# A four-layer graph network on one core: layer 1's ends cut finer, layer 2's first block as a dense sum

## The chip, the cores and the metric

One core of a Trainium2 chip runs the whole program. The metric is the device time of one execution in microseconds; of several runs the median is given. The profile shows one execution, taken by the hardware profiler, and its time differs from the median of the runs.

## The reference

2708 nodes with 512 features each, and one sparse matrix `adj` of 2708 x 2708 (a diagonal, and some four neighbours in a row). Four layers follow each other, each a residual and a layer norm. What matters here are layers 1 and 2:

```python
def layer1(x, adj):                       # attention over neighbours, and a plain sum
    t  = adj @ x
    ga = sigmoid([t, x] @ Wa.T + ba);  gb = sigmoid([t, x] @ Wb.T + bb)
    h  = x @ W_sa
    e  = where(adj != 0, exp(-leaky_relu(s_left(h)[:, None] + s_right(h)[None, :], 0.01)), 0)
    return sigmoid(ga * ((e / (e.sum(1) + 1e-5)) @ h) + gb * (adj @ (x @ W_gcnb) + b_gcnb))

def layer2(x, adj):                       # weighted incidence
    head = (adj > 0) / max(sqrt((adj > 0).sum(1)), 1e-12)
    inc  = adj + head
    return (inc @ x) / inc.sum(1)

x = layernorm(x + layer0(x, adj))         # residual sum with a dense projection
x = layernorm(x + layer1(x, adj))
x = layernorm(x + layer2(x, adj))
x = layernorm(x + layer3(x, adj))         # degree-normed sum, projection, tanh
```

## The kernel before

Rows of the result are worked off in NB = 24 blocks of R = 113 rows (the last has 109). Layer 0 reads the whole of `adj`, block by block, and writes a list of the non-zero entries: for each block up to EC x 128 = 512 edges in four **chunks** of 128 edges, with the source node (`source`), row and value of each. From then on a sum over neighbours is done in two steps. `gather` (L602) issues four indirect DMAs on POOL for a block, one for each chunk, which fetch the rows of the source nodes from a table in device memory into one of three buffers `gath` (block i uses buffer i % 3). Then TensorE multiplies: a chunk's edge values, spread to a 128 x 113 matrix, against the chunk's fetched rows, summed over the four chunks in PSUM (`aggregate`, L614). The diagonal is kept apart and added from the block's own rows.

Each layer's result is written to a table (`table[1]` after layer 1) by DMAs from the SP queue, and the next layer's gathers wait until the table is complete, since a source may be any node.

The order of instructions on each engine is written out by hand: every engine takes its instructions strictly in the order of the program text, and waits by semaphores where an operand is late. So a call's place in the text is its place in the queues of all the engines that it uses. A buffer ring (`bufs=`) makes a write wait for the readers of the tile that had the place before.

The parts of layer 1 for block i, with their engines:

- `gather1(i)`: four gathers of 1029 columns on POOL from `table[0]`. `load_own1(i)` (L648) loads the block's own rows by SP for the first nine blocks, `gather_own1(i)` (L1394) by one indirect DMA on POOL for those after.
- `values1(i, chunks)`: ScalarE spreads the edge values (`edge_s`).
- `scores1(i)` (L1421): two VectorE steps and an exp on ScalarE on a [128, 4, 113] tile. They need all four chunks. `mask1(i)` (L1432) zeroes what is no edge. `s_left` (L1377, L1383) holds the left scores of all blocks, spread over the partitions by transposes on TensorE and a VectorE copy for four blocks at once; all six are made before the loop.
- `sums1(i)` (L1436) and `scored_sums1(i)` (L1446): 8 matmuls each, two column halves of four chunks, half after half; `l1s` and `l1e` in the profile.
- `gates1`, `gated1`, `both1` (L1482), `stats1` (L1504), `scale1`, `norm1`: VectorE and ScalarE, with a small power on POOL (L1523); `norm1` stores the block to `table[1]`.
- `source_sum(i)` (L1349): one VectorE step for the degrees that layer 3 needs; it uses `in_block` and `block_of`. `row_norms` (L1592) makes the norm of the rows for layer 2: three VectorE steps and a power on POOL.

The loop interleaves blocks: in turn i it gathers block i + 2, sums block i, finishes block i - 1 and scores block i + 1.

Between the layers: `turn_norm` and `copy_norm` spread a row norm over the partitions (TensorE, ScalarE), `values` (L1304) and `incidence` (L1622) make the edge weights of layer 2 on VectorE for blocks 0 and 1, `keep_warm` (L1579) issues matmuls whose result is not read, and a chain of small VectorE steps (L1697 to L1730) makes the row sums and degrees. Then layer 2 gathers blocks 0 and 1 (L1714), and its loop runs over the 24 blocks: gather of block i + 2, `aggregate` of block i (`l2a`), `stats2` and `norm2` of block i - 1, `values` and `incidence` of block i + 2. `own2(i)` makes the block's own part, which has the diagonal and the residual.

Of the kernel before, what the change touches and what calls it, by code (L numbers as in the profile page):

```python
# [12 lines left out]
P = 128  # L13
# [6 lines left out]
EC = 4  # L20
# [427 lines left out]
def sparse_stack(  # L448
# [213 lines left out]
    with ExitStack() as phase:  # L662
# [635 lines left out]
        for i in range(7, NO):  # L1298
            load_own1(i)
# [29 lines left out]
    for k, t in enumerate((ba_bc, bb_bc)):  # L1329
# [7 lines left out]
    in_block = gpool.tile([P, NB, NS], I32, name="in_block")  # L1337
    nc.vector.tensor_scalar(
        in_block, where_all, 1.0 / R, 0.5 / R - 0.5, op0=ALU.mult, op1=ALU.add
    )  # L1340
    block_of = gpool.tile([P, NB, NS], FP, name="block_of")
    for g, (c0, _) in enumerate(SEGS):
        at = slice(8 * g, 8 * g + 8)
        nc.vector.tensor_scalar(
            block_of[:, :, at], in_block[:, :, at], float(c0), None, op0=ALU.add
        )
# [74 lines left out]
    def scores1(i):  # L1421

        e = spool.tile([P, EC, R], FP, tag="e", name=f"e{i}")
        nc.vector.tensor_tensor(
            e, gath[i % NGB][:, :, SR : SR + 1].to_broadcast([P, EC, R]),
            over_chunks(s_left[:, i, :]), ALU.add,
        )
        nc.vector.scalar_tensor_tensor(e, e, 0.01, e, op0=ALU.mult, op1=ALU.max)
        nc.scalar.activation(e, e, AF.Exp, scale=-1.0)
        edge_e[i] = e  # L1430

    def mask1(i):  # L1432
        e = edge_e[i]
        nc.vector.scalar_tensor_tensor(e, edge_s[i], 0.0, e, op0=ALU.is_gt, op1=ALU.mult)

    def sums1(i):  # L1436
        g, s, r = gath[i % NGB], edge_s.pop(i), rows(i)
        sum_s[i] = ps_1s.tile([P, 2, D], FP, tag="s1", name=f"l1s{i}")
        for k, at in enumerate(s_at):
            for c in range(EC):  # L1440
                nc.tensor.matmul(  # L1441
                    sum_s[i][:r, k, : at.stop - at.start], lhsT=s[:, c, :r], rhs=g[:, c, at],
                    start=(c == 0), stop=(c == EC - 1),
                )

    def scored_sums1(i):  # L1446
        g, e, r = gath[i % NGB], edge_e.pop(i), rows(i)
        sum_e[i] = ps_1e.tile([P, 2, D], FP, tag="e1", name=f"l1e{i}")
        for k, at in enumerate(e_at):
            for c in range(EC):  # L1450
                nc.tensor.matmul(  # L1451
                    sum_e[i][:r, k, k : k + at.stop - at.start], lhsT=e[:, c, :r],
                    rhs=g[:, c, at], start=(c == 0), stop=(c == EC - 1),
                )
# [27 lines left out]
    def both1(i):  # L1482
# [9 lines left out]
        nc.vector.scalar_tensor_tensor(  # L1492
            halves(va, r), halves(own1.pop(i)[:, 1 : D + 1], r), ediag[:r, i : i + 1],
            agg[:r, :, 1 : H + 1], op0=ALU.mult, op1=ALU.add,
        )
        v = work.tile([P, D], FP, tag="v", name=f"l1v{i}")
        nc.vector.scalar_tensor_tensor(
            v[:r, :], va[:r, :], rec[:r, :], vb1.pop(i)[:r, :], op0=ALU.mult, op1=ALU.add
        )

        nc.scalar.activation(v[:r, :], v[:r, :], AF.Tanh, scale=0.5)
        v1[i] = v

    def stats1(i):  # L1504
        r, v = rows(i), v1[i]
        nc.vector.scalar_tensor_tensor(
            v[:r, :], v[:r, :], 0.5, xr[:r, i, :], op0=ALU.mult, op1=ALU.add
        )
        stats = small.tile([P, 6], FP, tag="stats", name=f"st_l1_{i}")
        nc.vector.bn_stats(stats[:r, :], v[:r, :])  # L1510
# [4 lines left out]
        nc.vector.bn_aggr(mv[:r, k, 0:2], stats[:r, :])  # L1515
# [74 lines left out]
    nc.vector.tensor_scalar(plus, adiag, 0.0, None, op0=ALU.is_gt)  # L1590
# [17 lines left out]
    row_in, inc2 = {}, {}  # L1608
# [21 lines left out]

    b3_bc = gpool.tile([P, D], FP, name="b3_bc")
# [4 lines left out]
    gather1(1)  # L1636
    values1(1, range(EC))
    for i in range(0, NB, 4):
        spread_left(i)
    spread_bias(bg_bc)  # L1640
    scores1(0)
    mask1(0)
    for i in range(NB):
        if i + 2 < NB:
            gather1(i + 2)
        sums1(i)
# [4 lines left out]
        scored_sums1(i)  # L1651
        if i + 1 == NB:
            turn_norm(0)
            turn_norm(1)
        if i + 1 < NB:
            scores1(i + 1)
# [17 lines left out]
        if i + 1 == NB:  # L1674
            nc.sync.dma_start(out=b3_bc[0:1, :], in_=b3[None, :])
            nc.sync.dma_start(out=w3_sb, in_=w3T.rearrange("(b p) o -> p b o", p=P))
        if i < KB:
            source_sum(i)
        if i == KB:
            source_sums_out()  # L1680
            row_norms(slice(0, KB))
    copy_norm(0)
    copy_norm(1)
    keep_warm(ps_sp, "sp", [P, 4, P], 8)
    both1(NB - 1)
    spread_row(b3_bc, "b3")
    stats1(NB - 1)
    scale1()
    norm1(NB - 1)
    deg_ps = source_sums_in()  # L1690
    inc_s = [values(0)]
    incidence(0, inc_s[0])
    inc_s.append(values(1))
    incidence(1, inc_s[1])
# [11 lines left out]
    phase.close()  # L1706
    ps_agg = ctx.enter_context(tc.tile_pool(name="ps_agg2", bufs=2, space=bass.MemoryType.PSUM))
    ps_tr = ctx.enter_context(tc.tile_pool(name="ps_tr2", bufs=1, space=bass.MemoryType.PSUM))
    ps_o = ctx.enter_context(tc.tile_pool(name="ps_o2", bufs=2, space=bass.MemoryType.PSUM))
    ps_sp = ctx.enter_context(tc.tile_pool(name="ps_sp2", bufs=2, space=bass.MemoryType.PSUM))  # L1710
    ps_u = ctx.enter_context(tc.tile_pool(name="ps_u", bufs=1, space=bass.MemoryType.PSUM))


    for i in range(2):  # L1714
# [210 lines left out]
```

## Time and profile before

| | |
|---|---|
| median of 3 runs | 973.66 us (972.88 to 977.18) |
| the profiled execution's own time | 958.69 us |
| its span | 956.9 us |
| busy: TensorE, VectorE, ScalarE, POOL | 884.8, 685.3, 526.3, 465.5 us |
| layer 0 | to about 410 us |
| layer 1 | first gather 414.26, last norm ends 615.2 |
| layer 2 | first gather 618.51, last matmul ends 753.9 |
| layer 3 | first gather 760.79, to the end |

Times in the traces are microseconds from the start of the span. A row of a timeline has the start, the duration (us), the engine (PE is TensorE, DVE VectorE, ACT ScalarE, POOL GpSimd), the line of the kernel, the operation, the output and inputs by name, the count of instructions merged in the row, and in brackets the idle time before with what ended it. A 32-bit matmul is recorded as two passes, so x8 are four matmuls. A row of DMA_INDIRECT is the issuing of a gather on POOL, not its transfer; that ends some microseconds later ("to landing").

### The profile page before, as it was taken

The numbers are of one execution on the slowest core, as the hardware profiler recorded it, in microseconds if no ns is written. First come the engines' busy times: TensorE is split into PE (matmuls) and PEld (weight loads), VectorE is DVE, ScalarE is ACT, GpSimd is POOL, SyncE is SP. The second block draws the span as 40 slices with busy tenths as digits, with TensorE's granted clock in tenths as the row PEclk, the third lists the DMA queues.
The fourth block names the chain that finished last, engine by engine and source line by source line (L and its number), as shares of the span: only waits on it lengthen the run. The fifth ranks groups of instructions, "written<-read, shape, count | busy, mean of one in ns | idle before, by whom it ended". The sixth has DMA issues, their size and how long they took to land.

```text
span 956.9 us, 11163 instructions
## 1 busy us (share of the span) xinstructions
PE 884.8 (92%) x2957; PEld 489.4 (51%) x2957; DVE 685.3 (72%) x1811; ACT 526.3 (55%) x1221; POOL 465.5 (49%) x518
## 2 busy tenths in 40 slices
PE   6889999999999999989999999798888899999993
PEld 2446565556565565557777777433233334444441
DVE  7788798888888853148999999777777436565553
ACT  5776676867677672347777777344544312222221
POOL 3323131432323230057777753377777477766630
PEclk7879999999999999989999999989999999999997
DMA  9986887988878454388999976367777466555531
GB/s 245 323 208 184 216 229 207 272 223 220 227 206 238 152 166 126 115 286 292 349 330 342 341 276 236 95 188 213 212 218 217 131 170 189 163 174 162 151 107 32
DMA packets 133717, 201.73 MB, mean 211 GB/s; under 512 B 82658, under 2 KB 82704, under 8 KB 133647
## 3 DMA queue, kind: packets, MB, share of 16 engines
q0 software_dynamic: 39024, 118.69, 40.2%
q1 hardware_dynamic: 94623, 82.25, 30.2%
q8 instruction: 26, 0.43, 0.2%
q14 instruction: 44, 0.36, 0.1%
HBM read 182.81 MB, written 27.80 MB: 220 GB/s over the span
## 4 chain that ended last, share of the span: by engine, by line
PE 58%; DMA 14%; DVE 14%; issue 5%; ACT 4%; SPq 3%; POOL 2%; POOLq 0%; DVEq 0%; ACTq 0%
PE o_l L588 15%; DMA gath<-table,source 11%; PE l3a L617 8%; PE hb L588 7%; PE h L588 7%; PE l0a L617 6%; PE l2a L617 2%; PE fetched L929 2%; POOL gath L604 2%; PE unread L1585 2%; DVE l1b L1471 1%; SPq L691 1%; DMA gath<-in_x_dram 1%; DVE l1b L1475 1%; DVE l1a L1492 1%
## 5 line engine op out<-in xcount | busy, mean ns | idle before, releaser
L604 POOL DMA_INDIRECT gath<-table,source x288 | 305.0, 1059 | 102.7 <-issue 49.0
L604 POOL DMA_INDIRECT gath<-in_x_dram,source x96 | 97.4, 1015 | 224.9 <-issue 190.7
L617 PE MATMUL l2a<-gath,s_left 128*113 128x512 f32 (+1 forms) x192 | 97.2, 624 | 17.6 <-DMA gath<-table,source 17.4
L1451 PE MATMUL l1e<-gath,e 128*113 128x257 f32 (+3 forms) x384 | 88.4, 383 | 10.4 <-DVE l1a L1492 10.4
L617 PE MATMUL l3a<-gath,s 128*113 128x512 f32 (+1 forms) x192 | 88.3, 603 | 2.7 <-DMA gath<-table,source 2.7
L1441 PE MATMUL l1s<-gath,s 128*113 128x256 f32 (+3 forms) x384 | 89.8, 387 | 0.0
L617 PE MATMUL l0a<-gath,s 128*113 128x512 f32 (+1 forms) x192 | 87.5, 596 | 0.1
L588 PE MATMUL o_l<-shared,xi_own 128*113 128x512 f32 (+1 forms) x192 | 86.5, 593 | 0.8 <-ACT xi_own L581 0.7
L588 PE MATMUL hb<-w_gc_sb,xi_own 128*128 128x512 f32 (+1 forms) x176 | 83.3, 601 | 0.0
L1451 PEld LDWEIGHTS l1e<-gath,e 128*113 128x113 f32 (+1 forms) x384 | 66.2, 177 | 32.7 <-PE l1s L1441 19.4
L588 PE MATMUL o_l<-w_sb,uw_own 128*128 128x512 f32 (+1 forms) x176 | 82.7, 614 | 0.2
L588 PE MATMUL h<-w_sa_sb,xi_own 128*128 128x259 f32 (+1 forms) x352 | 80.8, 382 | 0.0
L1441 PEld LDWEIGHTS l1s<-gath,s 128*113 128x113 f32 (+1 forms) x384 | 69.2, 181 | 17.8 <-ACT s L1416 1.5
L588 PEld LDWEIGHTS h<-w_sa_sb,xi_own 128*128 128x128 f32 (+1 forms) x352 | 64.8, 185 | 19.8 <-issue 6.1
L617 PEld LDWEIGHTS l2a<-gath,s_left 128*113 128x113 f32 (+1 forms) x192 | 30.4, 181 | 73.9 <-DMA gath<-table,source 53.9
L1844 ACT ACTIVATE y<-l3v,mv_l 113x512 f32<-113x512 f32 (+1 forms) x24 | 19.5, 813 | 86.2 <-DVE mv_l L1840 79.2
L588 PEld LDWEIGHTS o_l<-shared,xi_own 128*113 128x113 f32 (+1 forms) x192 | 33.9, 177 | 49.2 <-issue 47.1
L617 PEld LDWEIGHTS l0a<-gath,s 128*113 128x113 f32 (+1 forms) x192 | 33.5, 179 | 40.7 <-issue 35.5
L617 PEld LDWEIGHTS l3a<-gath,s 128*113 128x113 f32 (+1 forms) x192 | 32.5, 180 | 41.2 <-issue 37.9
L1818 DVE SCALAR_TENSOR_TENSOR l3v<-o_l,d_inv,b_bc 113x512 f32<-113x512 f32 (+1 forms) x25 | 18.1, 728 | 48.1 <-PE o_l L588 48.1
L1308 DVE TENSOR_SCALAR s<-niota_r,nrow,edges 128x113 f32<-128x113 f32 x192 | 51.5, 344 | 0.0
L876 DVE FIND_INDEX8 where_all<-rec_all,shared 128x8 uint32<-128x678 f32 (+1 forms) x64 | 51.2, 800 | 0.0
(256 smaller groups left out, 1580.6 us busy)
## 6 DMA issues: line engine op xcount, KB each, us to landing
shared<-in_adj_dram SPq DMA_DIRECT2D x14, 1186.5 KB
table<-st SPq DMA_DIRECT2D x21, 514.5 KB
gath<-in_adj_dram SPq DMA_DIRECT2D x7, 1186.5 KB
gath<-in_x_dram SPq DMA_DIRECT2D x21, 256.0 KB
xi_own<-in_x_dram SPq DMA_DIRECT2D x23, 224.0 KB
table<-xr SPq DMA_DIRECT2D x23, 224.0 KB
table<-y SPq DMA_DIRECT2D x23, 224.0 KB
out_dram<-y SPq DMA_DIRECT2D x23, 224.0 KB
```

The lines of the kernel that those rows point to most:

```text
L588: nc.tensor.matmul(o, lhsT=uT[:, f, :r], rhs=w[:, f, :], start=(f == 0), stop=(f == DB - 1))
L604: nc.gpsimd.indirect_dma_start(out=g[:, c, :n], out_offset=None, in_=src[:, :], in_offset=bass.IndirectOffsetOnAxis(ap=source[:, i, c : c ...
L617: nc.tensor.matmul(agg[:r, :], lhsT=s[:, c, :r], rhs=g[:, c, off : off + D], start=(c == 0), stop=(c == EC - 1),)
L691: nc.sync.dma_start(out=a[:TAIL, NF, :r], in_=adjT[NF * P :, at])
L876: nc.vector.max_index(out=where_all[:, i, g * 8 : (g + 1) * 8], in_max=top, in_values=seg)
L929: nc.tensor.matmul(t["fetched"][:, c, : 3 * NS], lhsT=t["q"][:, c * P : (c + 1) * P], rhs=rec_all[:, i].rearrange("p k s -> p (k s)"), sta ...
L1308: nc.vector.tensor_scalar(s[:, c, :], niota_r, nrow[:, i, c : c + 1], edges[:, i, c, 1:2], op0=ALU.is_equal, op1=ALU.mult,)
L1441: nc.tensor.matmul(sum_s[i][:r, k, : at.stop - at.start], lhsT=s[:, c, :r], rhs=g[:, c, at], start=(c == 0), stop=(c == EC - 1),)
L1451: nc.tensor.matmul(sum_e[i][:r, k, k : k + at.stop - at.start], lhsT=e[:, c, :r], rhs=g[:, c, at], start=(c == 0), stop=(c == EC - 1),)
L1585: nc.tensor.matmul(o[:, :cols], lhsT=ident, rhs=bg_bc[:, :cols], start=True, stop=True)
L1818: nc.vector.scalar_tensor_tensor(v[:r, at], o[:r, at], d_inv[:r, i : i + 1], b3_bc[:r, at], op0=ALU.mult, op1=ALU.add,)
L1844: nc.scalar.activation(y[:r, :], v[:r, :], AF.Identity, bias=mv[:r, 3:4], scale=mv[:r, 2:3])
```

## The change

It has five parts.

1. **Start of layer 1.** The own rows of blocks 7 and 8 are no longer loaded by SP at the end of layer 0, but by `gather_own1` on POOL after the gathers of block 1. For block 0 `scores1` and `mask1` are called twice, for two chunks each, and the matmuls of `sums1` and `scored_sums1` go chunk by chunk, both halves of a chunk after each other. `in_block`, `block_of` and `plus` are made later, and two matmuls that nobody reads are added.
2. **`spread_left` late.** Only the first two of six calls stay ahead of the loop; the others are made in turns 1 to 4 of the loop.
3. **End of layer 1.** In turn 22 `load_all` loads the first 113 columns of the transposed `adj` (what block 0 needs, from all 2708 sources) by six SP DMAs into `xi_own` and `uw_own`, whose own rows are done with. Row norm of block 0: `row_norms(slice(0, 1))` at the end of turn 20, `turn_norm(0)` and `copy_norm(0)` in turn 21.
4. **Last block of layer 1 by halves:** `both1` and `stats1` work on two column halves of 256.
5. **Layer 2's first block.** `incidence_all` turns the loaded columns into weights on VectorE, four nodes' blocks at a time, and `sums_all` multiplies all 24 of them with `xr`, the rows as they lie in SBUF, into `l2all`; nothing is gathered for block 0. Its values hold the diagonal, so `own2(0)` has the factor 1. `values` and `incidence` are made for blocks 1 and 2, after that; the gathers ahead of the loop are those of blocks 1 and 2, and the loop starts at 1. Four `keep_warm` matmuls are left of eight, and the PSUM pools of layer 1 are closed after `stats2(0)`.

The diff, cut to its core:

```diff
         store0(KB - 1)
-        for i in range(7, NO):
-            load_own1(i)
...
+    def in_turn(i, parts):
+        both = [(k, at, c) for k, at in enumerate(parts) for c in range(EC)]
+        return sorted(both, key=lambda t: t[2]) if i == 0 else both
...
-    def both1(i):
+    def both1(i, parts=2):
...
+        for k in range(0, 2, parts):
+            kk, at = slice(k, k + parts), slice(k * H, (k + parts) * H)
...
-    def stats1(i):
+    def stats1(i, parts=1):
...
+    NX = xi_own.shape[1] // R
+    all_in = [
+        t[:, : n * R].rearrange("p (b i) -> p b i", i=R)
+        for t, n in ((xi_own, NX), (uw_own, NB - NX))
+    ]
+    def load_all():
+        for t, a, b in ((all_in[0], 0, NX), (all_in[1], NX, NB - 1)):
+            part = adjT[a * R : b * R, :R].rearrange("(b p) i -> p b i", p=R)
+            for at in (slice(0, R // 16 * 16), slice(R // 16 * 16, R)):
+                nc.sync.dma_start(out=t[at, : b - a, :], in_=part[at])
...
+    def incidence_all(blocks):
+        for b in blocks:
...
+            nc.vector.scalar_tensor_tensor(
+                inc[:R, :n, :], t[:R, at, :], 0.0,
+                row_in[0][:R, None, :].to_broadcast([R, n, R]), op0=ALU.is_gt, op1=ALU.mult,
+            )
+            nc.vector.tensor_add(t[:R, at, :], t[:R, at, :], inc[:R, :n, :])
+    def sums_all(blocks):
...
+            nc.tensor.matmul(
+                sum2[0][:R, :], lhsT=all_in[b >= NX][: rows(b), b - NX * (b >= NX), :],
+                rhs=xr[: rows(b), b, :], start=(b == 0), stop=(b + 1 == NB),
+            )
...
     gather1(1)
+    for i in (7, 8):
+        gather_own1(i)
     values1(1, range(EC))
-    for i in range(0, NB, 4):
+    for i in (0, 4):
         spread_left(i)
...
-    scores1(0)
-    mask1(0)
+    for at in (slice(0, 2), slice(2, EC)):
+        scores1(0, at)
+        mask1(0, at)
     for i in range(NB):
         if i + 2 < NB:
             gather1(i + 2)
+        if i + 2 == NB:
+            load_all()
         sums1(i)
...
         scored_sums1(i)
-        if i + 1 == NB:
+        if i == NB - 3:
             turn_norm(0)
+            copy_norm(0)
+        if i + 1 == NB:
             turn_norm(1)
+            turn_norm(2)
...
+        if 0 < i and 4 * i + 4 < NB:
+            spread_left(4 * i + 4)
         if i < KB:
             source_sum(i)
+        if i == NB - 4:
+            row_norms(slice(0, 1))
         if i == KB:
             source_sums_out()
-            row_norms(slice(0, KB))
-    copy_norm(0)
+            row_norms(slice(1, KB))
     copy_norm(1)
-    keep_warm(ps_sp, "sp", [P, 4, P], 8)
-    both1(NB - 1)
-    spread_row(b3_bc, "b3")
-    stats1(NB - 1)
+    copy_norm(2)
+    keep_warm(ps_sp, "sp", [P, 4, P], 4)
+    both1(NB - 1, 1)
+    stats1(NB - 1, 2)
+    incidence_all((0,))
     scale1()
     norm1(NB - 1)
+    for b in range(EC, 4 * EC, EC):
+        incidence_all((b,))
+    sums_all(range(3 * EC))
+    incidence_all((4 * EC, NX))
+    incidence_all(range(NX + EC, NB, EC))
+    sums_all(range(3 * EC, NX))
+    spread_row(b3_bc, "b3")
     deg_ps = source_sums_in()
-    inc_s = [values(0)]
-    incidence(0, inc_s[0])
-    inc_s.append(values(1))
-    incidence(1, inc_s[1])
+    sums_all(range(NX, NB))
+    inc_s = [values(1)]
+    incidence(1, inc_s[0])
+    inc_s.append(values(2))
+    incidence(2, inc_s[1])
...
-    for i in range(2):
+    for i in range(1, 3):
         gather(gath[i], i, table[1], D)
...
     own2(0)
-    for i in range(NB):
+    stats2(0)
+    own2(1)
+    phase.close()
...
+    for i in range(1, NB):
```

## The prediction

> **What bounds the kernel now.** I read the chain of waits first: it runs through layer 0 on TensorE, then in layers 1 and 2 through gathers and waits, so the change is judged stage by stage. Second the timeline of each engine around the three places that are edited.
>
> Layer 1, steady state (VectorE, then TensorE):
>
> ```profile
> 438.89 0.75 DVE L1471 SCALAR_TENSOR_TENSOR l1b<-shared,adiag,l1s 113x512 f32<-113x512 f32 x1 [0.32 <-ACT row_cnt L1465]
> 446.57 0.75 DVE L1471 SCALAR_TENSOR_TENSOR l1b<-shared,adiag,l1s 113x512 f32<-113x512 f32 x1 [0.32 <-ACT row_cnt L1465]
> ...
> 442.52 3.69 PE L1451 MATMUL l1e<-gath,e 128*113 128x257 f32 x16 [0.29 <-DVE l1a L1492]
> 450.30 3.69 PE L1451 MATMUL l1e<-gath,e 128*113 128x257 f32 x16 [0.61 <-DVE l1a L1492]
> ```
>
> VectorE idles 0.32 us in a block of 7.5 to 7.7 us, and that idle is a round trip to ScalarE, which no extra work fills; TensorE waits for VectorE in every block. **VectorE sets layer 1**: what is added to it lengthens the layer by its duration.
>
> The start of layer 1 hangs on POOL's gathers:
>
> ```profile
> 423.34 0.99 POOL L604 DMA_INDIRECT gath<-table,source  x1 [0.30 <-issue]
> 428.70 0.99 POOL L604 DMA_INDIRECT gath<-table,source  x1 [0.30 <-issue]
> ...
> 429.35 0.63 DVE L1424 TENSOR_TENSOR e<-gath,s_left 128x452 f32<-128x452 f32 x1 [2.46 <-DMA gath<-table,source]
> 435.69 0.63 DVE L1424 TENSOR_TENSOR e<-gath,s_left 128x452 f32<-128x452 f32 x1
> ```
>
> The first row is the last gather of block 1, the second the last of block 2. VectorE waits for block 1 until 429.35, and begins `scores1(2)` at 435.69 without a wait.
>
> The end of layer 1 (POOL, ScalarE, VectorE):
>
> ```profile
> 583.79 0.71 POOL L1523 TENSOR_TENSOR mv_l<-mv_l,root 113x2 f32<-113x2 f32 x1 [3.86 <-DVE gate L1461]
> 584.69 1.06 POOL L604 DMA_INDIRECT gath<-table,source  x1 [0.19 <-issue]
> 586.06 0.39 DVE L1352 SCALAR_TENSOR_TENSOR in_block<-block_of,rec_all 128x192 int32<-128x192 f32 x1
> 588.66 1.19 POOL L604 DMA_INDIRECT gath<-table,source  x1 [0.30 <-issue]
> 590.70 0.56 ACT L1429 ACTIVATE e<-e 128x452 f32<-128x452 f32 x1
> 591.56 0.75 DVE L1471 SCALAR_TENSOR_TENSOR l1b<-shared,adiag,l1s 113x512 f32<-113x512 f32 x1 [0.32 <-ACT row_cnt L1465]
> 595.82 0.62 DVE L1424 TENSOR_TENSOR e<-gath,s_left 128x452 f32<-128x452 f32 x1
> ```
>
> The gather of the last block (584.69 to 588.66) is issued before VectorE ends block 20 (586.46). Layer 2:
>
> ```profile
> 618.51 1.43 POOL L604 DMA_INDIRECT gath<-table,source  x1 [4.36 <-DMA table<-xr]
> 640.76 1.00 POOL L604 DMA_INDIRECT gath<-table,source  x1 [0.30 <-DMA gath<-table,source]
> 748.66 1.01 POOL L604 DMA_INDIRECT gath<-table,source  x1 [0.30 <-issue]
> ...
> 629.50 3.88 PE L617 MATMUL l2a<-gath,s_left 128*113 128x512 f32 x8
> 750.33 3.60 PE L617 MATMUL l2a<-gath,s_left 128*109 128x512 f32 x8
> ```
>
> These are the first of 96 gathers, the 17th (block 4) and the last. POOL never idles more than 0.31 us between them: **POOL's issuing sets layer 2**, 1.37 us each, 5.5 us a block.
>
> **What the skill says.** "TensorE: Matmul & The Clock Gate" (What's actually happening): the array runs at half clock after an idle window and needs some 3.4 us of work to come back. The trace agrees: after 3 us of idleness the matmuls that warm the clock at 609.96 start 0.85 us apart, from 614.3 on 0.43. "DMA: Bandwidth & Descriptors" (Issuing engines are not separate DMA queues): transfers from SP and POOL interleave on the same engines; here their share is 1.03 at 423 to 426 us (397 GB/s), so a moved load is not free in layer 1. The clock page again (Architectural detail: the array is 16× 32×32): ScalarE, VectorE and POOL are strictly first in, first out; the trace shows no overtaking, and the steps for the end of layer 1 rest on it.
>
> **Part 1, start of layer 1.** Four `load_own1` DMAs (two of 448 KB) leave SP at 411.4; own blocks 7 and 8 become two gathers on POOL behind block 1's. Splitting block 0 by chunks lets TensorE finish it earlier (half the `scores1` chain, and only two matmuls after the last chunk), but the next VectorE step waits for block 1, whose gathers keep their issue times: worth nothing by itself. Without the own loads block 1 may land up to 1.5 us sooner. Block 2's gathers go behind two issues of 1.3 us: its last issue moves from 428.70 to 431.3, and with the 5.9 us median to landing of this stretch (5.1 to 6.9) it lands at 437.2. `scores1(2)` moves from 435.69 to about 437.0: **+1.3 us** (0.7 to 2.5). Block 3 then lands near 443, wanted at 445: POOL has caught up. The later `in_block`, `block_of` and `plus` (1.5 us) lie in VectorE's wait for block 0, as they did: nothing, while that wait of 1.5 us and more lasts.
>
> **Part 2, spread_left in the loop.** Of six s_left copies (624 ns each by the row of L1383) four move from before the loop, where VectorE waited for the gather, into blocks 1 to 4, where it doesn't: 4 x (0.624 + 0.03) = **+2.65 us**. Their transposes (0.47 us a block; 0.94 for two sets at 413.48) fit in TensorE's 0.3 to 0.6 us of waits. Two added warm-up matmuls lie before block 0's gather has landed: nothing.
>
> **Part 3, end of layer 1.** `row_norms(0:1)` at the end of block 20: three VectorE instructions, **+0.6** (the same three took 601.31 to 601.91). Its power on POOL stands ahead of block 23's gathers, so they wait for VectorE: start at 586.46 + 0.6 + 0.1 + 0.55 + 0.2 = 587.9 instead of 584.69, 3.2 late. `copy_norm(0)` on ScalarE is put ahead of block 22's exp and waits for a transpose behind block 21's matmuls, which end at 591.25 (592.0 with what precedes). Exp then starts 592.55 against 590.70 + 0.6, and the gate and row_cnt copies behind it are what VectorE waits for: **+1.35**. So `scores1(23)` wants its gather at 597.8. Before, the DMA engines ran dry at 593.0, 4.4 after the last issue; now 591.9 + 4.4 = 596.3, but SP runs ahead and sends the 1.2 MB of adj at about 588.8. That cost about 4.3 us of full DMA share in layer 0 (near 280 GB/s), so landing comes at 597 to 599: **+0.4** (0 to 1.5). The adj is used only at 614.9. Its six issues delay only block 20's store behind them on SP. Sum of parts 1 to 3: +6.3.
>
> **Part 4, last block by halves.** Layer 3's last block has the rows: 256 columns take 0.43 to 0.44 where 512 take 0.69 to 0.75. Eight halves (3.4 us plus gaps) replace four wholes with a ScalarE tanh between: 0 within 0.3. `incidence_all((0,))`, 1.3 us, is put in the 0.76 us gap before `scale1`: block 23's store comes 0.6 us later. That is on no path, as follows.
>
> **Part 5, layer 2.** The dense sum is 24 matmuls of 128x512 shape, 3.43 / 4 = 0.86 us each warm: 20.6, plus the b3 row and the deg turn, 1.0. It can start when `incidence_all((0,))` ends, 614.9 (times of before; all shift by part 1 to 3). Four warm-up matmuls end at 614.8, so the clock is up. End 636.5. VectorE has 8 us of incidence, 4.8 for blocks 1 and 2 and 4.9 for the late values; it ends by 636, in time. The gathers of blocks 1, 2 and 3 (12 issues from 619.1) are out at 635.5, and nothing waits for them: TensorE is last. Block 4's first gather reuses block 1's buffer by chunk: 636.6 + 1.0 = 637.6, against 640.76. Thereafter POOL is the bound as before, TensorE catching up at 4.4 us a block. **-3.1 us** (-1 to -4.8; the whole four issues would be 5.4). Closing the pools later adds no wait in the compiled order; layer 3 only shifts.
>
> **Sum.** +1.3 + 2.65 + 0.6 + 1.35 + 0.4 - 3.1 = +3.2 us on the profiled execution's 958.69 (span 956.9). The median of the runs is 973.66, 15 us above that execution; I add the same 3.2: **976.9 us**. That is +0.33%; 0.5% (4.9 us) is about what a measurement can tell from no change.
>
> **Rivals.** (a) *Slower*: the last gather of layer 1 is caught between POOL's power and the adj load. If the adj is served first, its 4.3 us are added to 591.9 and layer 1's usual 6.9: 603 against 597.8, 5.2 us of VectorE waiting in place of 0.4, total +8, 981.7. It decides from a landing at 599.9 on. For it: SP runs ahead, and the DMA share is full while gathers land. Against it: the two interleave and the DMA was dry from 593. (b) *TensorE cold*: if the dense sum begins after a gap, its first 3.4 us run at half clock, 1.7 lost, and the gain shrinks to 1.4 or less: +4.9 to +6, 979. For it: the sum comes 1 us after a 3 us idle stretch has been made good; against: four matmuls filled that stretch exactly. (c) *Hidden costs*: block 1 lands earlier and VectorE spends the copies in waits that I count as fixed, block 2 is in time, and all four issues are gained: +1.5 - 5.4, 970. For it: POOL's full row; against: 0.32 us of idleness a block has no room. (d) *Nothing*: gain and costs of 3 cancel; it lies within the forecast.
>
> **Chances.** Forecast with (d) 0.57, (a) 0.22, (b) 0.11, (c) 0.10. Faster by over 0.5%: half of (c), whose value lies just inside, and 0.03 of the forecast, 0.08. Slower: 0.20 of (a), half of (b) and 0.08 of the forecast's upper bounds, 0.34. The rest, 0.58, is the same. Range 971.0 to 982.0: it takes in (a), (b) and the upper part of (c), and the bounds of parts 1 and 5.
>
> **What would show it.** `scores1(2)` waits for its gather near 437; l1e starts lie 8.1 us or more apart in blocks 1 to 4; block 23's first gather starts after VectorE's row_norms; exp of block 22 waits for the row_in copy; `l2all` runs some 21 us without a gap; the first gather of block 4 starts after TensorE's first l2a, POOL idle about 2 us before it. Wrong: VectorE with a wait over 1 us in blocks 5 to 20, a gather of block 1 or 2 in layer 2 that TensorE waits for, or a dense sum at half clock.

## The result, and the profile after

In 20 runs of each on one chip the changed kernel took 979.07 us (median) and the kernel before 976.12: a ratio of 1.0028, 95% interval 1.0010 to 1.0047. In a second set it took 960.55 us and the kernel before 958.09: a ratio of 1.0032, 1.0017 to 1.0048. So the change costs some 3 us, less than the half per cent that counts as a difference here.

One thing must be known ahead of the traces. The kernel before took 976.1, 971.9, 958.8 and 958.1 us in the four timed sets; a comparison holds only within a set. The first profile of before (span 956.9) has the length of the 958 us sets, although the three timed runs beside it have a median of 973.66; the first profile of after (975.6) is of the 976 us set. Subtracting one from the other would charge the change with 19 us. A second profile of each stands beside them. In the table A is to be compared with D, and B with C, with more care, since B is of the 972 us set and C of the 976 us set; times are us from the start of one event to the start of the next, and rec is the first small VectorE step that reads l1e.

| stretch | A before (956.9) | D after, second (958.3) | B before, second (968.2) | C after, first (975.6) |
|---|---|---|---|---|
| first gather of layer 1 to rec of block 6 | 65.18 | 68.22 | 65.58 | 70.82 |
| to rec of block 19 | 99.14 | 99.23 | 99.13 | 100.03 |
| to rec of block 23 | 30.26 | 31.57 | 30.24 | 31.57 |
| to the norm1 of block 23 | 5.54 | 5.78 | 5.54 | 5.78 |
| to layer 2's first gather | 4.13 | 3.96 | 4.13 | 3.96 |
| to layer 2's last l2v | 135.46 | 133.98 | 140.75 | 140.31 |
| to layer 3's first l3u | 15.75 | 16.26 | 15.48 | 16.24 |
| to layer 3's last l3u | 165.08 | 164.55 | 171.65 | 169.61 |

A to D: layer 1 up to its last norm +4.7 us, layer 2 -1.5 (from its first gather to its last l2v), the rest -0.2: +3.0, which agrees with the ratios. Layer 3 is untouched and moves by 0.5 at most in this pair. The table begins at layer 1's first gather. What lies before took 414.26 us in A and 412.58 in D, and 410.97 to 415.97 over all fourteen profiles, in no order by kernel; that is why the spans of A and D differ by 1.4 only.

The start of layer 1, timeline of the second profile of after (POOL, VectorE, TensorE):

```profile
424.27 0.99 POOL L1384 DMA_INDIRECT xi_own<-table,own_at  x1 [0.30 <-issue]
429.66 0.99 POOL L604 DMA_INDIRECT gath<-table,source  x1 [0.30 <-issue]
...
434.87 0.63 DVE L1414 TENSOR_TENSOR e<-gath,s_left 128x452 f32<-128x452 f32 x1 [0.57 <-DMA gath<-table,source]
440.07 0.62 DVE L1371 COPY s_left<-sl 128x452 f32<-128x452 f32 x1
...
442.23 3.69 PE L1445 MATMUL l1e<-gath,e 128*113 128x257 f32 x16 [1.09 <-DVE l1a L1490]
450.56 3.69 PE L1445 MATMUL l1e<-gath,e 128*113 128x257 f32 x16 [0.77 <-DVE l1a L1490]
```

The first row is the second own gather, the next the last gather of block 2 (17.08 us after the first gather of the layer, 14.44 before). It lands 5 us after its issue, and scores1(2), which had no wait before, now has one of 0.57. An s_left copy stands in VectorE's queue, and TensorE waits longer for VectorE: the starts of l1e lie 8.66, 8.33, 8.00 and 8.34 us apart from block 1 to block 5, where they were 7.46, 7.78, 7.47 and 7.77.

The end of layer 1, the same view (POOL, ScalarE, VectorE, SP):

```profile
588.41 0.55 POOL L1599 TENSOR_TENSOR inv_norm<-inv_norm,root 128x1 f32<-128x1 f32 x1 [2.45 <-DVE rec L1480]
589.12 1.07 POOL L604 DMA_INDIRECT gath<-table,source  x1 [0.17 <-issue]
593.31 0.99 POOL L604 DMA_INDIRECT gath<-table,source  x1 [0.30 <-PE l1e L1445]
...
593.41 0.26 ACT L1617 COPY row_in<-sp_in 128x113 f32<-128x113 f32 x1 [0.75 <-PE sp_in L1611]
594.32 0.75 DVE L1465 SCALAR_TENSOR_TENSOR l1b<-shared,adiag,l1s 113x512 f32<-113x512 f32 x1 [1.21 <-ACT row_cnt L1459]
598.58 0.62 DVE L1414 TENSOR_TENSOR e<-gath,s_left 128x452 f32<-128x452 f32 x1
...
588.49 9.50 SPq L569 DMA_DIRECT2D table<-xr  x4
598.15 2.37 SPq L1641 DMA_DIRECT2D xi_own<-in_adj_dram  x2
```

Block 23's gathers start behind the power, as forecast, and the row_in copy stands ahead of block 22's exp; VectorE's wait for row_cnt grows from 0.32 to 1.21. But scores1(23) at 598.58 waits for no gather, and SP sends the adj only at 598.15. In SP's queue the stores of blocks 18 and 19 stand in front of it (the row of four issues, 588.49 to 597.99), and block 19's rows are ready only at about 597.

Layer 2, the same view (TensorE, POOL):

```profile
617.96 15.62 PE L1665 MATMUL l2all<-xr,xi_own 113*113 113x512 f32 x36
634.58 5.41 PE L1665 MATMUL l2all<-xr,uw_own 113*113 113x512 f32 x12
640.91 3.69 PE L617 MATMUL l2a<-gath,s_left 128*113 128x512 f32 x8 [0.82 <-DVE l2v L1810]
...
621.34 1.08 POOL L604 DMA_INDIRECT gath<-table,source  x1 [4.32 <-DMA table<-xr]
636.67 0.99 POOL L604 DMA_INDIRECT gath<-table,source  x1 [0.30 <-issue]
642.30 1.09 POOL L604 DMA_INDIRECT gath<-table,source  x1 [4.63 <-PE l2a L617]
```

The dense sum runs 22 us, with the b3 row and the turn of deg in it, and needs 0.43 us per recorded pass (15.62 / 36), the pace that the prediction read for the warm array. Then the first l2a waits 0.82 us for stats2(0). The last two POOL rows are the 12th gather and the 13th, block 4's first: 4.63 us of idleness, and 20.96 us after the first gather, where block 4's stood at 22.25 before. From there to the last l2v it takes 113.0 us, before 113.2. This last stretch scatters: with the same layer-2 code it took 112.6 to 115.3 us in the five profiles of 957 to 963 us, so that block 4's gather (20.4 to 21.0 us in the four of them that gather the own rows by POOL) is a surer measure of the gain than the end of the layer.

### The profile page after: what moved, and what is told of

It reads as the page before. It is cut to its first block, busy times and chain, and to the rows that moved or that the text cites. A ratio compares the mean times of both kernels' runs of the same rounds, so it can differ in the third digit from the quotient of the medians.

```text
span 975.6 us, 11226 instructions
## 1 busy us (share of the span) xinstructions
PE 895.3 (92%) x2991; PEld 499.7 (51%) x2991; DVE 691.7 (71%) x1829; ACT 525.9 (54%) x1223; POOL 463.3 (47%) x517
## 4 chain that ended last, share of the span: by engine, by line
PE 64%; DVE 12%; issue 6%; DMA 5%; POOL 4%; ACT 3%; SPq 2%; another core or an unknown queue 2%; POOLq 0%; DVEq 0%; ACTq 0%
PE o_l L588 15%; PE l3a L617 8%; PE l2a L617 8%; PE hb L588 7%; PE h L588 7%; PE l0a L617 6%; POOL gath L604 3%; PE unread L1584 3%; PE l2all L1665 2%; PE fetched L929 2%; DMA gath<-table,source 2%; DMA gath<-in_x_dram 1%; SPq L691 1%; PE tr_l L1080 1%
## 5 line engine op out<-in xcount | busy, mean ns | idle before, releaser
L604 POOL DMA_INDIRECT gath<-table,source x284 | 299.5, 1055 | 115.9 <-issue 69.1
L1445 PE MATMUL l1e<-gath,e 128*113 128x256 f32 (+3 forms) x384 | 91.2, 392 | 15.6 <-DVE l1a L1490 10.4
L1436 PE MATMUL l1s<-gath,s 128*113 128x261 f32 (+3 forms) x384 | 90.8, 390 | 1.9 <-DMA gath<-table,source 1.9
L1445 PEld LDWEIGHTS l1e<-gath,e 128*113 128x113 f32 (+1 forms) x384 | 68.3, 182 | 38.3 <-issue 16.0
L617 PE MATMUL l2a<-gath,s_left 128*113 128x512 f32 (+1 forms) x184 | 85.3, 606 | 0.8 <-DVE l2v L1810 0.8
L1584 PE MATMUL unread<-bg_bc,ident 128*128 128x512 f32 x70 | 37.1, 640 | 18.4 <-remote 13.3
```

The costliest lines, as they stand in the source:

```text
L604: nc.gpsimd.indirect_dma_start(out=g[:, c, :n], out_offset=None, in_=src[:, :], in_offset=bass.IndirectOffsetOnAxis(ap=source[:, i, c : c ...
L617: nc.tensor.matmul(agg[:r, :], lhsT=s[:, c, :r], rhs=g[:, c, off : off + D], start=(c == 0), stop=(c == EC - 1),)
L1436: nc.tensor.matmul(sum_s[i][:r, k, : at.stop - at.start], lhsT=s[:, c, :r], rhs=g[:, c, at], start=(c == 0), stop=(c == EC - 1),)
L1445: nc.tensor.matmul(sum_e[i][:r, k, k : k + at.stop - at.start], lhsT=e[:, c, :r], rhs=g[:, c, at], start=(c == 0), stop=(c == EC - 1),)
L1584: nc.tensor.matmul(o[:, :cols], lhsT=ident, rhs=bg_bc[:, :cols], start=True, stop=True)
```

## The experiments

Edits are against the changed kernel. Ratios are to the kernel before in the same set; where no ratio is given there was one run and its profile, and only stretches are compared.

### Second profiles of both kernels

> The kernel before, unchanged, for a second profile of it. Theory A (the first profile of before, 956.9 us, was one of its shortest executions, and its layers 2 and 3 are shorter there than they usually are): ratio 1.000 within 0.002, span of this profile 970 to 978, the surplus over 956.9 lies in layers 2 and 3 as waits for gathers (layer 2 about 5 to 12 us more than 135 us from its first gather to the end of its last l2a, layer 3 about 4 to 5 more than 170), layer 1 as it was. Rival B (the first profile of before is typical, and the changed kernel really loses 5 us in layer 2 and 4.5 in layer 3): span within 3 us of 957.

Measured: 970.99 us, ratio 0.9991 (0.9969 to 1.0013), span 968.2, a little under A's range. Layer 1 as in the first profile (column B), layer 2 5.3 us longer, layer 3 6.6 longer, more than A said. Theory A in kind; B, a span near 957, falls. The list of waits of this run, from 612 us on (us in total, times, longest):

```profile
PE unread L1585 <- remote: 14.1, 4, 6.8
PE l2a L617 <- DMA gath<-table,source: 3.8, 4, 2.3
```

TensorE stands still four times, up to 6.8 us. "remote" means that the trace has no record of what ended the wait. All five profiles from the longer sets lack some 40% of the records of DMA landings (about 7 thousand, in the other nine 11 thousand), so that these are waits for gathers is likely but only argued.

> The changed kernel, unchanged, for a second profile on the same chip as the next two kernels. Theory A (stage by stage from the runs so far): first gather of layer 1 to rec of block 6 takes 68.2 to 70.8 us (65.2 and 65.6 before), rec of block 19 to rec of block 23 takes 31.57 (30.25), VectorE's row_cnt wait in block 22 is 1.2 us, the first l2a waits 0.82 us for stats2(0), block 4's first gather starts 20.4 to 20.7 us after layer 2's first (22.25 and 21.95 before), ratio 1.003 to 1.005. Rival B (the wait of 1.58 us on rec of block 0 and the cold matmuls of block 1 in the first profile belong to every execution): 70.8 us again, l1e of block 1 takes 6.6 us.

Measured: 960.55 us, ratio 1.0032 (1.0017 to 1.0048). Column D: theory A in all points (block 4's gather at 20.96, a quarter of a microsecond above the range). What the first profile of after shows at the start of layer 1 is not in it:

```profile
436.79 0.16 DVE L1480 SCALAR_TENSOR_TENSOR rec<-l1e,ediag 113x1 f32<-113x1 f32 x1 [1.58 <-remote]
...
438.15 6.58 PE L1445 MATMUL l1e<-gath,e 128*113 128x257 f32 x16 [3.92 <-DVE rec L1483]
```

There rec of block 0 waited 1.58 us, TensorE idled 3.92 us behind it, and then needed 6.58 us for matmuls of 3.69, with a granted clock of 0.50: the cold clock that "TensorE: Matmul & The Clock Gate" of the Trainium skill (What's actually happening) describes. The wait of rec stands in this profile alone. The slow matmuls of block 1 come twice more, shorter, in two of the runs below: in halves 5.37 us after 2.52 us of idleness, and in norms_moved 5.33 after 2.40:

```profile
436.72 5.33 PE L1445 MATMUL l1e<-gath,e 128*113 128x257 f32 x16 [2.40 <-DVE l1a L1490]
```

After 2.08 us (no_spread) they took 3.69. The page speaks of an idle window of some 3.4 us; here 2.40 us without a matmul were followed by the half clock. All three profiles with slow matmuls have block 0 by chunks, and none of the seven profiles with block 0 whole has such slow matmuls. In norms_moved they cost nothing: rec of block 6 comes 68.24 us after the first gather, in D 68.22.

### Parts 1 and 2: the start of layer 1

```diff
-    for i in (0, 4):                     # no_spread: part 2 back
+    for i in range(0, NB, 4):
         spread_left(i)
...
-        if 0 < i and 4 * i + 4 < NB:
-            spread_left(4 * i + 4)
```

> The changed kernel with part 2 taken back: all six s_left copies ahead of the loop. Theory A (VectorE sets layer 1, so each copy in the loop costs its 0.62 us): layer 1 is 2.5 to 2.7 us shorter than in the changed kernel, total about +0.5 us against before (ratio 1.0005). Rival B (the copies lie in waits that the later gather of block 2 makes anyway): layer 1 as long as in the changed kernel, ratio 1.003.

Measured: ratio 1.0021 (0.9999 to 1.0043), which can't part the theories. Nor can the layer's length: up to its last norm it is 204.98 us, 3.2 shorter than column C with its slow start, but no shorter than column D (204.80); here rec of block 0 comes late, 22.67 us after the first gather (19.64 in D). What tells is the spacing of the l1e starts from block 1 to block 5: 7.48, 7.79, 7.47 and 7.78 us, as before the change. So the copies lengthen these blocks: theory A in its mechanism, B falls, and the 2.5 us of the layer were not seen.

```diff
         store0(KB - 1)                   # own_on_sp
+        for i in range(7, NO):
+            load_own1(i)
...
-    for i in (7, 8):
-        gather_own1(i)
```

> The changed kernel with the rows of own blocks 7 and 8 loaded by SP ahead of layer 1 again, and no longer by POOL between the gathers of blocks 1 and 2. Theory A (these two gathers make block 2's late): layer 1 is 1.3 us shorter than in the changed kernel, 0.7 to 3 with TensorE's cold matmuls of block 1 (6.58 us in the changed kernel) at full clock; ratio to before 1.001 to 1.002. Rival B (the halves of block 0 are what delays the start, or nothing does): block 1 is as late, TensorE idles near 4 us ahead of l1e of block 1 as in the changed kernel, ratio 1.003.

Measured: ratio 1.0033 (1.0014 to 1.0053), layer 1 204.65 us, 3.55 shorter than C but only 0.15 shorter than D. scores1(2) waits for no gather, where it waits 0.57 to 0.90 us in D, norms_moved and adj_earlier; on the other hand rec of block 0 waited 0.66 us for TensorE. TensorE's l1e of block 1 takes 3.69 us, after 1.9 us of idleness. So A is right in the place, its 1.3 us were not seen, and the ratio is B's. A possible reason shows only in layer 2: see the last section.

```diff
     # halves: both edits above, so of part 1 only block 0 by chunks is left
     # own_whole: no_spread's edit, and
-        return sorted(both, key=lambda t: t[2]) if i == 0 else both
+        return sorted(both, key=lambda t: t[2]) if i < 0 else both
...
-    for at in (slice(0, 2), slice(2, EC)):
-        scores1(0, at)
-        mask1(0, at)
+    scores1(0)
+    mask1(0)
```

> Layer 2 and the end of layer 1 as in the changed kernel, the copies of s_left ahead of the loop, own blocks 7 and 8 by SP; of part 1 only block 0 by chunks is left. Theory A (worth nothing, VectorE waits for block 1 anyway): first gather to rec of block 0 takes 20.0 to 20.4 us (20.37 in the run without it, 19.45 and 19.84 in the two of before), layer 1 202.5 to 203.2. Rival B (it saves what TensorE is earlier by, 0.5 to 1 us): 19.4 us or less, layer 1 below 202.2.

Measured: rec of block 0 at 19.52 us, between the two of before; layer 1 203.78. All four ranges are missed. The excess lies in one wait of 1.26 us for the gather of block 5, and in 0.4 us at the end; neither is near block 0. scores1(1) waits 2.48 us for block 1's gather and starts 15.16 us after the first gather, in before 2.46 and 15.09: what block 0 gains ends there. So block 0 by chunks is worth nothing that can be seen, as A says.

> As in the run with block 0 by chunks alone, but the other half of part 1: block 0 whole, own blocks 7 and 8 gathered by POOL behind block 1. Theory A (the own gathers alone delay the start): first gather to rec of block 0 takes 21.7 to 22.7 us and layer 1 about 205, as where both are in. Theory B (they delay only block 2, as the prediction had it): rec of block 0 at 20.0 to 20.4 us, scores1(2) waits about 1.3 us for its gather, layer 1 about 204.1. Rival C (chunk order and own gathers hurt only together): 202.8.

Measured: rec of block 0 at 20.01 us, and, in the timeline of VectorE:

```profile
435.99 0.63 DVE L1414 TENSOR_TENSOR e<-gath,s_left 128x452 f32<-128x452 f32 x1 [0.69 <-DMA gath<-table,source]
```

First gather to rec of block 6: 66.54 us, against 65.10 in the run best (below, same set) without the own gathers. So they cost 1.4 us here: scores1(1) starts 0.68 us later, and scores1(2) waits 0.69. But the same stretch with the same code as in best took 65.15, 65.64 and 66.10 us in three other profiles, so the cost lies anywhere from 0.4 to 1.4. Theory B in the place, with half the wait that it named; the layer, 203.02 us, is nearer to C's 202.8 than to B's 204.1.

### What is left without parts 1 and 2

```diff
     # layer2_only: the edits of own_on_sp, no_spread and own_whole together
```

> The changed kernel with parts 1 and 2 taken back (own blocks 7 and 8 by SP, block 0 whole, all s_left copies ahead of the loop): what is left of the change is the end of layer 1 and layer 2. Theory A (the sum of the prediction): +2.35 for part 3 and -3.1 for part 5, -0.75 us against before, ratio 0.999. Rival B (layer 2 gains only half, because the first l2a waits for the end of stats2(0), 0.8 us, which the prediction did not have): +0.8 us, ratio 1.001. Rival C (layer 2 loses, as the two first profiles set side by side suggest): +5 us or more, ratio 1.005.

Measured: ratio 1.0020 (0.9998 to 1.0042). Layer 1 202.83 us, 2.3 above column B; layer 2 144.03 with waits of up to 5.3 us ("remote") as in column B. By the ratio nearest to B, by layer 2's stretch to C: undecided. In a set where these waits come and go, one profile can't show a gain of 1 to 3 us in layer 2; the runs below are of the 958 us sets.

### Part 3: the end of layer 1

```diff
-        if i == NB - 3:                  # norms_moved
+        if i + 1 == NB:
             turn_norm(0)
-            copy_norm(0)
-        if i + 1 == NB:
             turn_norm(1)
-            turn_norm(2)
...
-        if i == NB - 4:
+        if i == NB - 3:
             row_norms(slice(0, 1))
...
+    copy_norm(0)
+    turn_norm(2)
     copy_norm(1)
```

> The changed kernel with part 3's norm of block 0 out of the way: row_norms(0:1) one turn later (behind the last gathers of layer 1 on POOL), turn_norm(0) and copy_norm(0) after the last block's exp. Theory A (the copy ahead of exp of block 22 costs 0.9 us and the three VectorE steps 0.45): VectorE's wait of 1.21 us for row_cnt in block 22 goes back to 0.32, from rec of block 19 to rec of block 23 it takes 30.7 us in place of 31.57 (30.25 before), and block 23's first gather starts about 3 us earlier against the block it stands in; total +2.0 us against before, ratio 1.002. Rival B (that copy is not what VectorE waits for): 31.5 us again, ratio 1.003.

Measured: from rec of block 19 to that of block 23 it takes 30.70 us, and VectorE waits in block 22 as in other blocks:

```profile
596.30 0.75 DVE L1465 SCALAR_TENSOR_TENSOR l1b<-shared,adiag,l1s 113x512 f32<-113x512 f32 x1 [0.32 <-ACT row_cnt L1459]
```

So the copy ahead of exp costs 0.9 us; what is left to before, 0.45, are the three VectorE steps, which this run keeps. The ratio, 1.0044 (1.0027 to 1.0061), is above what was expected (1.002); layer 2 took 135.71 us here, 1.7 more than in column D with the same code, and mean issues of gathers of 1.09 us where D has 1.07. The stretch is shown, the total of +2.0 us is not.

```diff
-        if i + 2 == NB:                  # adj_earlier
+        if i + 4 == NB:
             load_all()
```

> The changed kernel with the adj load two turns earlier, so that SP sends it while the gathers of block 22 land (DMA share 0.93 to 0.95 there) and not after the last gather of layer 1 has landed. Theory A (the 1.2 MB fit beside the gathers without being waited for): VectorE waits under 0.3 us for a gather in blocks 21 to 23, rec of block 19 to rec of block 23 takes 31.57 us as in the changed kernel. Rival B (the price that the prediction's rival (a) named, 4.3 us of DMA time in front of a gather, is real once SP does send the load there): VectorE waits 1 to 4 us for block 22's gather, that stretch takes 32.5 us or more.

Measured: SP sends the load from 580.49 on, over the gathers of block 22; the DMA share is 1.02 and 1.13 in the two stretches of 5 us after 580. VectorE waits for no gather from 565 to 620 us (the list of its waits has two rows):

```profile
DVE l1b L1465 <- ACT row_cnt L1459: 3.3, 6, 1.2
DVE mv_l L1530 <- POOL mv_l L1522: 0.8, 1, 0.8
```

The stretch is 31.56 us: theory A. Transfers of SP and POOL interleave, as "DMA: Bandwidth & Descriptors" (Issuing engines are not separate DMA queues) has it, and 1.2 MB in front of a gather are not 4.3 us of delay. The room is small, though: block 23's last gather landed at 597.45, just ahead of scores1(23) at 597.48, where D had 0.68 us to spare. It took 5.24 us to land, in D 4.59, but 5.25 before the change, without any such load; so a small delay by the load is neither shown nor excluded.

### Layer 2

```diff
     # best: the edits of layer2_only and norms_moved, and
+    ps_o = ctx.enter_context(tc.tile_pool(name="ps_o2", bufs=2, ...))
+    ps_tr = ...
+    ps_u = ...
     ps_agg = ...                         # now behind ps_o, ps_tr and ps_u
```

> Only what pays by the runs so far: layer 2's dense sum with the last block by halves; parts 1 and 2 taken back; the norm of block 0 moved as in the run above; and layer 2's PSUM pools opened in another order, so that the first l2a no longer writes where stats2(0) still reads. Theory A: layer 1 201.2 to 202 us (200.1 and 200.5 before), the first l2a begins within 0.4 us of the end of the dense sum (0.82 us of waiting in the changed kernel), from layer 2's first gather to block 4's first 19.8 us (20.67 in the changed kernel, 22.25 before); net -1.0 to -2 us, ratio 0.998 to 0.999. Rival B (the dense sum gains nothing that layer 2's later waits for gathers don't take back): +1 us, ratio 1.001.

Measured: 959.43 us, ratio 1.0007 (0.9994 to 1.0021). Layer 1 up to its last norm 200.71 us (200.12 in column A): with parts 1 and 2 back and the norm moved, 0.6 is left of 4.7. The wait for stats2(0) is gone; yet block 4's gather is at 20.99 us, no earlier than in D (TensorE, POOL):

```profile
637.10 3.60 PE L617 MATMUL l2a<-gath,s_left 128*113 128x512 f32 x8
...
639.87 1.01 POOL L604 DMA_INDIRECT gath<-table,source  x1 [4.30 <-PE l2a L617]
```

The gather came 2.8 us after the start of the l2a whose first chunk it waits for, in D 1.4. Layer 2 took 135.46 us, as before the change. Neither theory: the edit did what it should, and the time was given back at the next step, of which the last section says more.

```diff
     sums_all(range(3 * EC, NX))          # l2a1_inside: best, and
+    for i in range(1, 3):
+        gather(gath[i], i, table[1], D)
+    inc_s = [values(1)]
+    incidence(1, inc_s[0])
     spread_row(b3_bc, "b3")
     deg_ps = source_sums_in()
+    sum2[1] = ps_1s.tile([P, 2, D], FP, tag="s1", name="l2a1")[:, 0, :]
+    first = inc2.pop(1)
+    for c in range(EC):
+        nc.tensor.matmul(
+            sum2[1][:R, :], lhsT=first[:, c, :R], rhs=gath[1][:, c, :D],
+            start=(c == 0), stop=(c == EC - 1),
+        )
     sums_all(range(NX, NB))
-    inc_s = [values(1)]
-    incidence(1, inc_s[0])
...
-    for i in range(1, 3):
-        gather(gath[i], i, table[1], D)
...
     for i in range(1, NB):
...
-        sum2[i] = aggregate(inc2.pop(i), gath[i % NGB], rows(i), f"l2a{i}")
+        if i > 1:
+            sum2[i] = aggregate(inc2.pop(i), gath[i % NGB], rows(i), f"l2a{i}")
```

> As the run called best, and in addition the sum of block 1 in layer 2 stands inside the dense sum (after its 18th block, in the second l1s buffer), so that block 4's gathers no longer wait for the end of the dense sum. Theory A (what eats the gain of layer 2 is that gather 13 waits for TensorE's l2a(1), which stands behind 21 us of dense sum; POOL's issuing sets the rest): POOL goes from gather 12 to 13 without the 4 us gap, block 4's first gather starts 15.9 to 16.9 us after layer 2's first, layer 2 is 3 to 4.5 us shorter than in the run best or in before, total 3 to 4 us below before, ratio 0.996 to 0.997. Rival B (the later waits of TensorE for gathers set layer 2, not the issues): block 4's gathers start earlier, but the layer ends as before, ratio 1.000.

Measured: 954.92 us against 958.09, ratio 0.9964 (0.9950 to 0.9977): below both kernels, though by less than the half per cent. TensorE and POOL:

```profile
634.53 3.69 PE L1768 MATMUL l2a<-gath,s_left 128*113 128x512 f32 x8
638.06 5.32 PE L1667 MATMUL l2all<-xr,uw_own 113*113 113x512 f32 x12
...
638.47 1.01 POOL L604 DMA_INDIRECT gath<-table,source  x1 [0.30 <-PE l2a L1768]
644.70 1.01 POOL L604 DMA_INDIRECT gath<-table,source  x1 [1.28 <-PE l2a L617]
```

The 13th gather follows the 12th without a gap, 17.02 us after the first (20.96 in D, and just above A's range); the small remaining gap has moved to block 5, whose gather now waits for an l2a behind the rest of the dense sum. Layer 2 takes 131.52 us, 2.5 less than D and 3.9 less than A; the run below has the same code there and took 133.15. Theory A: what had eaten the gain was the order on TensorE.

```diff
-    both1(NB - 1, 1)                     # last_whole: l2a1_inside, and
-    stats1(NB - 1, 2)
+    both1(NB - 1)
+    stats1(NB - 1)
```

> As the run before it, with the last block of layer 1 whole again (part 4 taken back). Theory A (halves are worth nothing, 0 within 0.3): rec of block 23 to its norm1 takes 5.7 to 6.0 us (5.79 with halves, 5.54 in before, where incidence_all(0) does not stand in that stretch). Rival B (halves save the overlap of tanh with VectorE, about 0.6 us): 6.3 us or more.

Measured: 5.92 us from rec of block 23 to its norm1, 5.78 with halves. Theory A: the halves save 0.14 us. The rest of the way from 5.54 would be `incidence_all((0,))`, which stands in that stretch; no run takes it out.

## Why the prediction was right, point by point

The total was right, +3.2 us forecast and about +3 measured, because two terms were too large by nearly the same: layer 1 was forecast at +6.3 and costs 4.7, layer 2 at -3.1 and brings 1.5 (columns A and D). The mechanisms were right in the main; that the two errors of 1.6 us cancel is luck.

- **Start of layer 1, +1.3**: right in kind and place. Measured 0.86 at scores1(2), of which 0.57 is its wait for the gather; in own_whole 0.4 to 1.4 by block 6. That block 0 by chunks is "worth nothing by itself" was right (halves). That a TensorE which ends block 0 earlier can fall to half clock before block 1 was not foreseen; it was seen in three of the seven profiles with block 0 by chunks.
- **s_left copies, +2.65**: right in mechanism, a little large. The spacing of l1e in blocks 2 to 5 grew by 0.55, 0.53 and 0.57 us where only a copy was added: 2.2 for four. The term that was mis-sized is 0.624 + 0.03 for one (four of them are 2.62, rounded up to 2.65): a row's duration overlaps the start of the next row on VectorE (the copy at 440.07 lasts 0.62, in a full queue the next starts 0.54 later). "Perfetto Trace Analysis" of the Trainium skill (Optimizing Scalar/DVE Operations) says so: the write acknowledgement overlaps with the next instruction. The price of one more instruction in a full queue is the distance of starts, not the duration.
- **row_norms, +0.6**: 0.45, by the same overlap (587.79 to 588.24 from its first step to what follows).
- **copy_norm ahead of exp, +1.35**: right in mechanism, 0.89 measured (1.21 - 0.32), and gone in norms_moved. Its own steps give a delay of exp of 1.25 (592.55 - 591.30), not 1.35. Counted from rec of block 20 exp starts 1.00 later (5.32 us after it, 4.32 before), and 0.1 of that lies in a wait that ScalarE's gate copies had in any case.
- **Last gather and adj, +0.4**: nothing. The step that failed is "SP runs ahead and sends the 1.2 MB of adj at about 588.8": block 19's store stands in front of the load on SP, and the load went out at 598.15, when the last gather was in (597.90). So the collision of rival (a), the slower case, does not happen. In adj_earlier the load is sent while the gathers of block 22 land, and VectorE waits for no gather. That is not quite (a)'s case, which was about block 23's late gathers: nearly all of the load was sent before these were issued.
- **Halves, 0 within 0.3**: 0.14 gained by them, 0.24 lost in the stretch as a whole. Layer 2's first gather comes 0.07 us later against rec of block 23, not 0.6 as forecast for the store.
- **Layer 2, -3.1**: the mechanism is right, and the cap was named: the dense sum ends on TensorE, then block 4's gather can start, and from there on POOL sets the pace (113.0 against 113.2 us). What failed is its time: 637.6, 19.1 us after the first gather of before; it was 20.96. Of the 1.86, 0.65 is the dense sum's end (18.65 against 18.0), 0.82 the wait of the first l2a for stats2(0), and 0.39 the way from the l2a to the gather (1.39 against 1.0). "Closing the pools later adds no wait" was the step that was wrong: the row of the first l2a shows a wait for the VectorE step that reads l2all, and with the pools opened in another order (best) it is gone. So the l2a must write a PSUM place that stats2(0) still reads. The gain of 1.5 at the layer's end rests on one pair of profiles; at block 4's gather it is 1.0 to 1.8 us (20.4 to 21.0 against 21.95 and 22.25). Nor was the price of the queue seen as what it is: the dense sum stands in front of an l2a that POOL needs, and l2a1_inside shows that moving this one sum ahead is worth more than the term in dispute.
- **Rival (b), TensorE cold**: the dense sum ran at 0.43 us a pass on the average, which leaves no room for a stretch at half clock. **Rival (c), hidden costs**: the copies are seen in the spacing. All signs of the forecast came, two not in size: POOL's idleness ahead of block 4 is 4.6 us, not 2, and one spacing of l1e is 8.00, not 8.1 or more.

## What to carry to other kernels

Work that is taken off the bounding engine (here 4 of 96 gather issues on POOL) only pays if what replaces it on another engine does not stand in front of the next thing that the bounding engine waits for: put the sum that frees a buffer ahead of the rest of the long one. What is added to a full queue costs the distance between starts; what is moved out of a wait into a full queue is paid for in every instance. Two profiles can be subtracted only if the same unchanged kernel takes the same time in both of their sets; a stretch that the change does not touch is the check. And a difference of one pair of profiles is worth no more than the scatter of that stretch between profiles of the same code.

## What was not expected of the hardware

- The kernel before took 958 to 976 us from one set of runs to another. In its two profiles (956.9 and 968.2) nearly all of the difference lies in layers 2 and 3: layer 1 200.1 and 200.5 us, layer 2 135.5 and 140.8, layer 3 165.1 and 171.7. In the longer one TensorE stands still up to 6.8 us at a time. Why is open. The sets were run on different chips as far as they are named (971.9 us on chip 7, 958.8 on chip 12, 958.1 on chip 1), and whether the chip is the cause was not tried; and the traces of the longer sets lack 40% of the records of landings.
- From the start of l2a to the start of the gather that waits for its first chunk it took 1.39 us in the second profile of after, 1.38 in own_whole, but 2.77 in best and 2.86 in halves. It goes with part 1: 1.38 or 1.39 us in all six profiles where POOL gathers the own rows of blocks 7 and 8, 2.77 to 2.86 in all four where SP loads them and block 1's l2a stands behind the whole dense sum. No row of another engine explains it, and how two gathers more in layer 1 do this was not tried. It is the reason why best gained nothing at block 4's gather. If those two gathers are the cause, part 1 has a return that nobody reckoned with: what they cost at the start of layer 1 is no more than what they save here. That would fit the ratio of own_on_sp, which is no lower with the two gathers taken back.
